# Layer 1 of a four-layer convolution-style kernel: first pieces loaded as attention drains, fifteen shared slots, planes stored raw and scaled by selecting products

## The chip, the cores and the metric

The kernel runs on one core of one Trainium2 chip. The metric is device time in microseconds (us) for one execution, lower is better. The engines are named as the profile names them: PE (matrix products; PEld is its weight load), DVE, ACT and POOL (elementwise work; ACT has the lookup functions), and SP, which issues most DMAs. "SPq", "POOLq" and so on are the queues of instructions of those engines.

## The reference

The input x is 1x256x256x128 f32. Four layers follow each other; each is `x = x + layer(_gn(x))`, where `_gn` is a group normalisation over 32 groups of 4 channels and the whole image. Layer 0 is an attention over rows with a triangle bias, layer 2 a gated triangle product over 128 channels, layer 3 a chain of small convolutions. The change is in layer 1, a gated triangle product over 16 channels:

```python
def _L1_conv_ref(x, Wa1, ba1, ..., Wz, bz):
    a = sigmoid((x @ Wa1 + ba1) * (x @ Wa2 + ba2))      # 256x256x16
    b = sigmoid((x @ Wb1 + bb1) * (x @ Wb2 + bb2))      # 256x256x16
    g = sigmoid(x @ Wg + bg)                            # 256x256x128
    z = einsum('bikc,bkjc->bijc', a, b)                 # per channel a 256x256 product
    return g * (_ln(z, ln2_g, ln2_b) @ Wz + bz)         # _ln over the 16 channels
```

## The kernel before, in words

All intermediate images lie in DRAM with the channel first: x1T (the input of layer 1), x2T (its output), abD (32 rows: 16 planes of a and 16 of b), znD (16 normalised planes of z). A token is one pixel; 65,536 tokens are cut into 32 pieces of SC = 2048 tokens, a piece into four chunks of CK = 512. A piece of x1T is an SBUF tile of 128 channels x 2048 tokens, 1 MB.

**Attention (layer 0)** works in 64 groups of four image rows, in a hand-written order (a `manual_schedule` loop over j). `gate` (L611) multiplies the gate in, takes the reciprocal of the softmax sums and sends it through DRAM (rzD) to spread it over the heads (L625, L628, issued by SP), `divide` (L636, POOL) multiplies, `output` (L643, L644) makes the new x, and `close` (L648, L650) takes bn_stats and stores the group to x1T by SP. The exponentials live in a pool p2e (six tiles of 8 KB per partition and five of 4 KB), which is opened after the pools p2c and p2.

**Between attention and layer 1** an aggregate of all statistics (L777) makes a flag, which every engine reads and branches on (`tc.If`, L787; the branch holds a slower attention for unusual numbers). Then `gn_finish` aggregates once more (L200) and folds the group normalisation into the weights of layer 1 (L207 to L219, L807 to L815). Only then are pieces of x1T loaded.

**Planes (L820 to L838).** For each piece in order: load (L824, SP), eight products that put four chunks into the four 32-partition quarters of a PSUM tile (L829), an Identity on ACT (L834), a fused multiply on DVE (L835), a Sigmoid on ACT (L837), and one store of 256 KB into abD by POOL (`store_groups`, L172). Eight of the 32 pieces stay in SBUF (`held`); the others go through three slots.

**Multiply (L850 to L893).** For each of 16 channels: load planes a and b in groups of four channels (L859, L861), turn a by four transposes (`tri_turn`, L1718, with a copy by ACT, L1720), multiply (`tri_multiply`, L1729), subtract the first plane (L870, DVE), square (L872, ACT), and add the sum and the sum of squares on POOL (L877, L878). All 16 results stay in SBUF. Afterwards variance, root and reciprocal (L882 to L886) give one factor per token, which scales all planes (L889, DVE, four instructions); then they are stored to znD (L890).

**Gating (L895 to L950).** For each piece: two halves of the gate product (L927) with a Sigmoid each (L930, ACT), four products of the normalised planes with Wz, each reading 16 partitions (L935), a fused add and multiply (L941, DVE, twice), the residual add on POOL (L944), then four bn_stats (L910, DVE) for the next group normalisation and the store to x2T (L911, SP). `fetch_zn` (L903) loads the normalised planes for four pieces in four transfers into 16 partitions each. Pieces that were not held are loaded again (L846), seven slots in all.

The time line of SP matters: it issues its DMAs in program order, and waits at each for the slot, the data or an earlier transfer.

The group normalisation that follows (`gn_finish(stats2)`) aggregates 128 statistics; layer 2 begins with loads of x2T (L999).

Of the kernel before, what the change touches and what calls it, by code (L numbers as in the profile page):

```python
# [9 lines left out]
F32 = mybir.dt.float32  # L10
AF = mybir.ActivationFunctionType
ALU = mybir.AluOpType
# [20 lines left out]
def kernel(ctx: ExitStack, tc: tile.TileContext, a: dict, out: bass.AP):  # L33
# [47 lines left out]
    cen4 = const.tile([P, 4, 32], F32, name="f1_c")  # L81
    nc.vector.memset(cen4, -1.0 / 16)
    for q in range(4):
        for sign, base in ((1, -32 * q), (-1, 32 * q + 31)):
            nc.gpsimd.affine_select(
                out=cen4[:, q, :], in_=cen4[:, q, :], compare_op=ALU.is_ge, fill=0.0, base=base,
                pattern=[[0, 32]], channel_multiplier=sign,
            )
    nc.vector.tensor_tensor(cen4.rearrange("p q c -> p (q c)"), cen4.rearrange("p q c -> p (q c)"), ident, ALU.add)
# [45 lines left out]
    wz4 = const.tile([P, D], F32, name="wz4")  # L135
    nc.vector.memset(wz4, 0.0)
    g4 = const.tile([P, 1], F32, name="g4")
    nc.vector.memset(g4, 0.0)
    for q in range(4):
        nc.gpsimd.dma_start(wz4[32 * q : 32 * q + 16, :], a["L1_conv_Wz"])  # L140
        nc.gpsimd.dma_start(g4[32 * q : 32 * q + 16, :], a["L1_conv_ln2_g"].unsqueeze(1))
# [28 lines left out]
    def store_groups(queue, dst, s, src):  # L170

        queue.dma_start(dst[:, s * SC : (s + 1) * SC].rearrange("c (q t) -> q c t", q=4), src)  # L172

# [23 lines left out]
    def gn_finish(stats, name):  # L197

        mv = const.tile([P, 2], F32, name=name + "_mv")
        nc.vector.bn_aggr(mv, stats.rearrange("p n s -> p (n s)"))  # L200
        return gn_groups(mv, name)

    def gn_groups(mv, name):
# [40 lines left out]
    wzc = const.tile([P, D], F32, name="wzc")  # L244
# [4 lines left out]
    with tc.tile_pool(name="x0", bufs=1) as xres, tc.tile_pool(name="p0", bufs=3) as sb:  # L249
        held = {s: xres.tile([P, SC], F32, name=f"x0_{s}") for s in range(RES, NSC)}  # L250
        with tc.tile_pool(name="p0ps", bufs=3, space=PSUM) as ps, tc.tile_pool(
# [12 lines left out]
            def folds():  # L264
# [37 lines left out]
                pw = fps.tile([P, D], F32, name="f1_w", tag="f0")  # L302
                nc.tensor.matmul(pw, lhsT=cen4.rearrange("p q c -> p (q c)"), rhs=wz4, start=True, stop=True)
                yield
                nc.vector.tensor_copy(wzc, pw)
# [186 lines left out]
    with tc.tile_pool(name="p2c", bufs=1) as cs:  # L492
        triT = cs.tile([P, NH, 2, N], F32, name="triT")
        with tc.tile_pool(name="p2", bufs=2) as sb, tc.tile_pool(name="p2e", bufs=6) as eb, tc.tile_pool(
# [117 lines left out]
            def gate(i0):  # L612
# [10 lines left out]
                nc.vector.reciprocal(rz, t["z"])  # L623
                for h in range(NH):
                    nc.sync.dma_start(rzD[g, h * G : (h + 1) * G, :], rz[h * HC : h * HC + G, :])  # L625
                rb = sb.tile([P, GT], F32, name="p2_rb")
                for h in range(NH):
                    nc.sync.dma_start(  # L628
                        rb[h * HC : (h + 1) * HC, :],
                        rzD[g, h * G : (h + 1) * G, :].rearrange("r n -> (r n)").unsqueeze(0).to_broadcast([HC, GT]),  # L630
                    )
# [14 lines left out]
            def close(g, c):  # L646
                x1 = groups[g]["x"]
                nc.vector.bn_stats(stats1[:, g * 2 + c, :], x1[:, c * CK : (c + 1) * CK])  # L648
                if c == 1:
                    nc.sync.dma_start(x1T[:, g * GT : (g + 1) * GT], x1)  # L650
                    del groups[g]
# [60 lines left out]
            for j in range(2 * NG + 5):  # L712
# [55 lines left out]
                if half == 0 and 0 <= g - 2 < NG:  # L768
                    divide(g - 2)
                if half == 1 and g + 2 < NG:  # L770
                    prepare(g + 2)


    flag = const.tile([P, 1], mybir.dt.int32, name="flag")
    with tc.tile_pool(name="chk", bufs=1) as sb, tc.tile_pool(name="chkps", bufs=1, space=PSUM) as ps:
        mv = sb.tile([P, 2], F32, name="chk_mv")
        nc.vector.bn_aggr(mv, stats1.rearrange("p n s -> p (n s)"))  # L777
        ok = sb.tile([P, 2], F32, name="chk_ok")
        nc.vector.tensor_scalar(ok, mv, 0.0, 0.0, ALU.mult, ALU.is_equal)
# [6 lines left out]
    with tc.If(again > 0):  # L786
# [4 lines left out]
        )  # L791

    layer0.close()
    m1, r1 = gn_finish(stats1, "gn1")

    v1 = const.tile([P, 32], F32, name="v1")
# [16 lines left out]
    stats2 = new_stats("stats2")  # L816
    R1 = 8
    with tc.tile_pool(name="x1", bufs=1) as xres, tc.tile_pool(name="xs1", bufs=3) as xsb:
        held = {s: xres.tile([P, SC], F32, name=f"x1_{s}") for s in range(0, NSC, NSC // R1)}
        with tc.tile_pool(name="p3", bufs=3) as sb, tc.tile_pool(name="p3ps", bufs=3, space=PSUM) as ps:  # L820
            for s in range(NSC):
                ss = slice(s * SC, (s + 1) * SC)
                xt = held[s] if s in held else xsb.tile([P, SC], F32, name="p3_x", tag="xs")
                nc.sync.dma_start(xt, x1T[:, ss])  # L824
                p1 = ps.tile([P, CK], F32, name="p3_1")
                p2 = ps.tile([P, CK], F32, name="p3_2")
                for pp, w in ((p1, v1), (p2, v2)):
                    for c in range(4):
                        nc.tensor.matmul(  # L829
                            pp[32 * c : 32 * c + 32, :], lhsT=w, rhs=xt[:, c * CK : (c + 1) * CK],  # L830
                            start=True, stop=True,
                        )
                s1 = sb.tile([P, CK], F32, name="p3_s1")
                nc.scalar.activation(s1, p1, AF.Identity, bias=vb1)  # L834
                nc.vector.scalar_tensor_tensor(s1, p2, vb2, s1, ALU.add, ALU.mult)  # L835
                ab = sb.tile([P, CK], F32, name="p3_ab", bufs=10)
                nc.scalar.activation(ab, s1, AF.Sigmoid)  # L837
                store_groups(nc.gpsimd, abD, s, ab)  # L838

        loaded = {}  # L840

        def fetch1(pool, tag, bufs):
            for s in range(NSC):
                if s not in held and s not in loaded:
                    loaded[s] = pool.tile([P, SC], F32, name="p4_x", tag=tag, bufs=bufs)
                    nc.sync.dma_start(loaded[s], x1T[:, s * SC : (s + 1) * SC])  # L846
                    return


        with tc.tile_pool(name="z", bufs=1) as zb, tc.tile_pool(name="zs", bufs=2) as sb, tc.tile_pool(  # L850
            name="zps", bufs=2, space=PSUM
        ) as ps:
            Z = zb.tile([P, 16, 2 * N], F32, name="Z")
            s1 = zb.tile([P, 2 * N], F32, name="z_s1")
            s2 = zb.tile([P, 2 * N], F32, name="z_s2")
            base = zb.tile([P, 2 * N], F32, name="z_base")
            for q in range(4):
                A = sb.tile([P, 4, 2 * N], F32, name="z_A")
                nc.sync.dma_start(A, abD[4 * q : 4 * q + 4, :].rearrange("c (p t) -> p c t", p=P))  # L859
                B = sb.tile([P, 4, 2 * N], F32, name="z_B")  # L860
                nc.sync.dma_start(B, abD[16 + 4 * q : 20 + 4 * q, :].rearrange("c (p t) -> p c t", p=P))  # L861
                for c in range(4):
                    at = tri_turn(nc, ps, sb, A, c, ident, nc.scalar.copy)
                    pz = tri_multiply(nc, ps, at, B, c).rearrange("p t n -> p (t n)")
                    k = 4 * q + c
                    if k == 0:
                        nc.vector.tensor_copy(base, pz)
                        nc.vector.memset(Z[:, 0, :], 0.0)
                        continue
                    nc.vector.tensor_tensor(Z[:, k, :], pz, base, ALU.subtract)  # L870
                    sq = sb.tile([P, 2 * N], F32, name="z_sq", bufs=3)
                    nc.scalar.activation(sq, Z[:, k, :], AF.Square)  # L872
                    if k == 1:
                        nc.gpsimd.tensor_copy(s1, Z[:, k, :])
# [896 lines left out]
```

## Time and profile before

| what | value |
|---|---|
| runs of the kernel, median of 4 | 3441.0 us (3435.27 to 3448.64) |
| profiled execution, its own time | 3431.01 us |
| profiled execution, span | 3429.3 us |
| mean granted PE clock | 0.958 |
| busy share PE / DVE / ACT / POOL | 91% / 68% / 57% / 48% |
| last bn_stats of attention ends | 1478.2 us |
| first product of the planes | 1499.6 us |
| first load of the multiply stage | 1610.6 us |
| last plane of z subtracted | 1658.2 us |
| first fused multiply of the gating | 1688.3 us |
| last store of layer 1 landed | 1864.6 us |

The last six rows are times from the start of the span in the profiled execution. Layer 1 thus takes about 386 us from the end of attention to the landing of its last store, 11% of the span. In the profile's groups a line gives the instruction's line and engine, the tile it writes and those it reads, the shape, the number of instructions, their busy time and mean duration, and how long the engine was idle just before them and what ended that. In the chain of waits, each step is followed back to what released it. "issue" is time in which the engine waited for nothing that the profile shows.

### The profile page before, as it was taken

Reading aid. Unit: us, or ns where it says so; the run is one execution under the profiler, and the core shown is the slowest. Engines: PE = TensorE matmul, PEld = TensorE weight load, DVE = VectorE, ACT = ScalarE, POOL = GpSimd, SP = SyncE. Lnnn points to the kernel's source line nnn. Section 1 sums busy time; section 2 is a strip of 40 time slices with the busy share of each in tenths; the row PEclk is TensorE's granted clock in tenths of the full one; section 3 lists DMA queues with packets and bytes.
Section 4 is the critical chain, followed back from the end, with each engine's and each line's share of the span. In section 5 each row is a group of like instructions: output and inputs, shape, how many; then the busy total and the mean of one; then the engine's idle time right before and its main releaser. Section 6 shows DMA issues by size and latency. Waiting matters only on the chain.

```text
span 3429.3 us, 52490 instructions
## 1 busy us (share of the span) xinstructions
PE 3113.6 (91%) x20266; PEld 1646.4 (48%) x20266; DVE 2318.3 (68%) x2635; ACT 1954.9 (57%) x2140; POOL 1650.4 (48%) x914
## 2 busy tenths in 40 slices
PE   6669999999999999955696999999999999859998
PEld 5425555555555555512432444444899533324444
DVE  5627888888888888831596445544555677747876
ACT  3657777777777777623343444543444466736555
POOL 4146777777777777721595000000555344514433
PEclk8889999999999999988898999999999999979999
DMA  9982333333333333279699676856999899856764
GB/s 391 358 292 80 118 117 110 119 106 120 111 119 107 118 114 111 95 271 346 194 324 355 233 273 250 311 217 232 344 351 350 307 336 334 305 161 196 208 198 130
DMA packets 302409, 755.31 MB, mean 220 GB/s; under 512 B 79577, under 2 KB 150139, under 8 KB 252363
## 3 DMA queue, kind: packets, MB, share of 16 engines
q1 hardware_dynamic: 288235, 741.02, 61.7%
q0 software_dynamic: 13920, 10.87, 1.1%
q8 instruction: 162, 2.65, 0.3%
q14 instruction: 92, 0.75, 0.1%
HBM read 464.09 MB, written 287.66 MB: 219 GB/s over the span
## 4 chain that ended last, share of the span: by engine, by line
PE 41%; DMA 9%; DVE 2%; issue 1%; ACT 1%; POOL 1%; SPq 0%; ACTq 0%; DVEq 0%; POOLq 0%
PE p_pm L1063 13%; PE tp_z L1729 7%; PE p_pm L1216 6%; PE p_pm L1451 5%; DMA p_x<-x1T 2%; DMA abD<-p_ab 2%; PE tp_a L1718 2%; DMA p_er<-eD 2%; DMA x2T<-p_x 2%; PE p_st L1020 1%; PE p_pt L1488 1%; PE p_eb L977 1%; PE p_rz L977 1%; PE p_rk L977 1%; PE p_pp L1344 1%
## 5 line engine op out<-in xcount | busy, mean ns | idle before, releaser
L575 DVE TENSOR_TENSOR p_e<-p_S,triT 128x1024 f32<-128x1024 f32 x512 | 609.4, 1212 | 144.4 <-PE p_S L565 144.4
L585 POOL TENSOR_TENSOR p_es<-p_e 128x1024 f32<-128x1024 f32 x256 | 602.9, 2366 | 125.6 <-issue 66.6
L583 ACT ACTIVATE p_e<-p_e,mbT 128x1024 f32<-128x1024 f32 x512 | 552.2, 1138 | 60.5 <-DVE p_e L575 60.3
L1063 PE MATMUL p_pm<-p_zn,wf 128*128 128x512 f32 x1040 | 450.8, 595 | 1.4 <-DVE p_zn L1080 1.4
L550 PE MATMUL p_mm<-p_xn,w 128*128 128x512 f32 x768 | 404.9, 610 | 0.3 <-DVE p_v L545 0.3
L1063 PEld LDWEIGHTS p_pm<-p_zn,wf 128*128 128x128 f32 x1040 | 197.8, 191 | 255.1 <-issue 248.3
L565 PE MATMUL p_S<-p_q,p_k 32*128 32x256 f32 x4096 | 295.1, 400 | 3.5 <-DVE p_e L575 3.3
L1465 POOL TENSOR_TENSOR p_q<-p_q,p_pb 128x2024 f32<-128x2024 f32 x32 | 144.1, 4504 | 251.3 <-DVE p_pb L1459 242.5
L565 PEld LDWEIGHTS p_S<-p_q,p_k 32*128 32x128 f32 x4096 | 185.9, 184 | 159.5 <-PE p_mm L541 91.7
L1129 POOL DMA_DIRECT2D rs__17885<-rs2D x4 | 2.0, 512 | 532.3 <-PE p_pm L1063 532.3
L1729 PE MATMUL tp_z<-p_B,tp_at 128*128 128x256 f32 x1024 | 250.7, 388 | 2.5 <-DMA p_B<-bD 2.2
L524 POOL TENSOR_TENSOR p_xn<-p_xn,p_rs 128x1024 f32<-128x1024 f32 x63 | 151.2, 2400 | 204.6 <-DMA p_rb<-rzD 122.8
L598 PE MATMUL p_o<-p_e,p_v 128*32 128x256 f32 x4096 | 247.6, 382 | 0.0
L1172 POOL TENSOR_TENSOR k<-k,p_sq 128x512 f32<-128x512 f32 x128 | 163.1, 1274 | 135.3 <-ACT p_sq L1170 135.3
L1282 POOL TENSOR_TENSOR p_x<-p_x,p_g 128x2048 f32<-128x2048 f32 x30 | 136.3, 4544 | 160.5 <-DVE p_g L1269 106.9
L1729 PEld LDWEIGHTS tp_z<-p_B,tp_at 128*128 128x128 f32 x1024 | 185.3, 191 | 25.2 <-issue 2.6
L550 PEld LDWEIGHTS p_mm<-p_xn,w 128*128 128x128 f32 x768 | 125.8, 190 | 104.3 <-issue 88.3
L1171 DVE TENSOR_TENSOR k<-tp_z,k 128x512 f32<-128x512 f32 x128 | 88.5, 692 | 129.0 <-ACT p_sq L1170 129.0
L598 PEld LDWEIGHTS p_o<-p_e,p_v 128*32 128x32 f32 x4096 | 120.0, 109 | 109.3 <-ACT p_g L556 41.5
L1096 DVE SCALAR_TENSOR_TENSOR p_b<-p_pm,b2w,p_b 128x1024 f32<-128x1024 f32 x64 | 82.2, 1284 | 125.6 <-PE p_pm L1063 111.2
L1168 ACT COPY p_K<-tp_z 128x512 f32<-128x512 f32 x128 | 74.9, 585 | 159.8 <-PE tp_z L1729 159.8
L541 PEld LDWEIGHTS p_mm<-w,p_xn 128*128 128x128 f32 x1024 | 134.4, 191 | 61.1 <-issue 60.1
(367 smaller groups left out, 5924.5 us busy)
## 6 DMA issues: line engine op xcount, KB each, us to landing
p_x<-x2T SPq DMA_DIRECT2D x64, 1024.0 KB
p_x<-x1T SPq DMA_DIRECT2D x48, 1024.0 KB
p_x<-in_x_dram SPq DMA_DIRECT2D x32, 1024.0 KB
p_x<-xT SPq DMA_DIRECT2D x64, 512.0 KB
p_rb<-rzD SPq DMA_DIRECT2D x256, 128.0 KB
x1T<-p_x SPq DMA_DIRECT2D x64, 512.0 KB
aD<-p_a SPq DMA_DIRECT2D x32, 1024.0 KB
bD<-p_b SPq DMA_DIRECT2D x32, 1024.0 KB
```

Source lines behind the costliest of these rows:

```text
L524: nc.gpsimd.tensor_tensor(xn, xn, groups[g]["rs"], ALU.mult)
L550: nc.tensor.matmul(pm, lhsT=w, rhs=t["xn"][:, cs_], start=True, stop=True)
L565: nc.tensor.matmul(Ss[h // 2][:, h % 2, u, :], lhsT=t["k"][hp, r * N + u * P : r * N + (u + 1) * P], rhs=t["q"][hp, r * N : (r + 1) * N], ...
L575: nc.vector.tensor_tensor(e[:, :, 2 * p : 2 * p + 2, :].rearrange("p u h n -> p h u n"), Ss[p], triT[:, 2 * p : 2 * p + 2, :, :], ALU.add,)
L583: nc.scalar.activation(e[:, u, :, :], e[:, u, :, :], AF.Exp, bias=mbT[:, u, i : i + 1])
L585: nc.gpsimd.tensor_tensor(es, e[:, 0, :, :], e[:, 1, :, :], ALU.add)
L598: nc.tensor.matmul(t["o"][hp, r % 2, :], lhsT=t["v"][:, r * 2 + u, hp], rhs=e[:, u, h, :], start=(u == 0), stop=(u == 1),)
L1063: nc.tensor.matmul(pm[:, c, :], lhsT=wf2[:, i, :], rhs=zns[s][:, k * CK : (k + 1) * CK], start=True, stop=True)
L1172: nc.gpsimd.tensor_tensor(k2, k2, sq, ALU.add)
L1216: nc.tensor.matmul(pm[:, c, :], lhsT=w, rhs=src[:, k * CK : (k + 1) * CK], start=True, stop=True)
L1451: nc.tensor.matmul(pm[:, 2 * c : 2 * c + 2, :], lhsT=w2c, rhs=src[:, r : r + 2, :], start=True, stop=True)
L1729: nc.tensor.matmul(pz[:, t, :], lhsT=at[:, u, t * P : (t + 1) * P], rhs=Bc[:, u, :], start=(u == 0), stop=(u == 1))
```

## The change

It does five things.

1. **Attention's end.** The pool p2e is opened first, so that it lies lowest. The last group's reciprocals and the last two groups' stores are issued by ACT instead of SP. The statistics of all groups but the last are aggregated inside the loop (`gn_part`), and merged with those of the last group by five small operations (`gn_merge`); flag and normalisation use the merged values. The first eight pieces of x1T are loaded ahead of the flag, into a pool that lies where p2e was.
2. **Slots.** Fifteen slots of 1 MB (KEEP = 10 and MORE = 5) hold pieces in planes, multiply and gating. Ten pieces stay from the planes on, five are loaded during the multiply, 17 during the gating, into a slot whose piece was stored. The order of the pieces alternates between the image's halves: 0, 16, 1, 17 and so on (`order1`).
3. **Planes.** The order is written by hand, with the Sigmoid one piece late. A piece is stored by four transfers of 32 partitions, two issued by POOL and two by SP, in another order of the tokens in abD, so that partition 32 q + s of a loaded plane holds chunk q of piece s.
4. **Multiply.** Planes come in groups of two channels, three groups ahead; the next plane is turned before the present one is multiplied; the sum goes to DVE (the sum of squares stays on POOL, the last on DVE). Each result is stored raw as soon as it is there.
5. **Gating.** The raw planes of four pieces are fetched in two transfers into 128 partitions. The factor per token is spread by small products with a selecting matrix (`spread`, eight products of 32x32 per four pieces), and a DVE multiply scales the planes. Statistics for the next normalisation come from the fused multiply's accumulation (DVE) and from a Square with accumulation on ACT, instead of bn_stats. For six of the pieces the residual add is done by DVE instead of POOL. Gates run two pieces ahead.

The core of the diff (the constants for Wz, with eight blocks of 16 rows instead of four, are cut):

```diff
-    with tc.tile_pool(name="p2c", bufs=1) as cs:
+    with tc.tile_pool(name="p2e", bufs=6) as eb, tc.tile_pool(name="p2c", bufs=1) as cs:
...
+                queue = nc.sync if g < NG - 1 else nc.scalar
                 for h in range(NH):
-                    nc.sync.dma_start(rzD[g, h * G : (h + 1) * G, :], rz[h * HC : h * HC + G, :])
+                    queue.dma_start(rzD[g, h * G : (h + 1) * G, :], rz[h * HC : h * HC + G, :])
...
+                    queue = nc.sync if g < NG - 2 else nc.scalar
+                    queue.dma_start(x1T[:, g * GT : (g + 1) * GT], x1)
...
+                if j == 2 * NG + 2:
+                    mv_first = gn_part(stats1, 0, 2 * NG - 2, "gn1_a")
...
+    order1 = [b + h * NSC // 2 for b in range(NSC // 2) for h in range(2)]
+    KEEP, MORE, FIRST = 10, 5, 8
...
+    for i in range(FIRST):
+        load1(i, x1_pool)
+    mv1 = gn_merge(mv_first, gn_part(stats1, 2 * NG - 2, 2 * NG, "gn1_b"), 1.0 - 1.0 / NG, "gn1_mv")
...
+            def store3():
+                s, ab = done.pop(0)
+                for q in range(4):
+                    (nc.gpsimd if q < 2 else nc.sync).dma_start(
+                        abD.rearrange("c (q s t) -> q s c t", q=4, t=CK)[q, s], ab[32 * q : 32 * q + 32, :]
+                    )
...
+                for k in range(16):
+                    if k and k % 2 == 0:
+                        load_z(k // 2 + 2)
+                    nxt = turn_z(k + 1)
+                    pz = tri_multiply(nc, ps, at, AB[k // 2][1], k % 2).rearrange("p t n -> p (t n)")
+                    at = nxt
...
+                            nc.vector.tensor_tensor(s1, s1, Z, ALU.add)
+                            (nc.vector if k == 15 else nc.gpsimd).tensor_tensor(s2, s2, sq, ALU.add)
...
+                            nc.sync.dma_start(znD[k_].rearrange("(p t) -> p t", p=P), Z_)
...
+                    if k % 2 == 1 and KEEP + k // 2 < KEEP + MORE:
+                        load1(KEEP + k // 2, xs_pool)
...
+                def scale_z(i):
+                    if i < NSC:
+                        rb = psg.tile([P, 2, CK], F32, name="p4_rb", tag="p4_pg")
+                        for m in range(2):
+                            for c in range(4):
+                                q = slice(32 * c, 32 * c + 32)
+                                nc.tensor.matmul(
+                                    rb[q, m, :], lhsT=spread[q, order1[i] + m, :], rhs=s1[q, :], start=True, stop=True
+                                )
+                        nc.vector.tensor_tensor(zs[i], zs[i], rb, ALU.mult)
...
+                def sum4():
+                    i = sums.pop(0)
+                    nc.scalar.activation(
+                        junk, xs[order1[i]], AF.Square, bias=c1neg, accum_out=qsum[:, i : i + 1]
+                    )
...
+                for i, s in enumerate(order1):
+                    xt = xs[s]
+                    if i:
+                        gate4(i + LEAD)
+                    if i % 4 == 0:
+                        fetch_z(i + 8)
+                    if i % 4 == 2:
+                        scale_z(i + 2)
...
+                            pzh if i in by_dve else gt[:, hs], pzh, bz, gt[:, hs], ALU.add, ALU.mult,
+                            accum_out=usum[:, 2 * i + h : 2 * i + h + 1],
...
+                    sums.append(i)
+                    if len(sums) > 1:
+                        sum4()
+                    if i:
+                        s_ = order1[i - 1]
+                        nc.sync.dma_start(x2T[:, s_ * SC : (s_ + 1) * SC], xs[s_])
+                    j = i - 3 + KEEP + MORE
+                    if i > 2 and j < NSC:
+                        load1(j, x1_pool if j % (KEEP + MORE) < KEEP else xs_pool)
```

## The prediction

> **What bounds layer 1 now.** I read the 40 slices first, then the busy time by stage, the groups between 1485 and 1870 us, the chain of waits, and the time line around each seam. All times are of the profiled execution: span 3429.3 us, time 3431.01 us. The median of the four runs is 3441.0, so I work out a difference and take it off both. A difference under 0.3% (10 us) counts as no change.
>
> Busy time by stage (PE, PEld, DVE, ACT, POOL, then granted clock, DMA share, GB/s):
>
> ```profile
> 1468.00:1500.00 32.00, 6.52 (x32) 3.73 (x36) 13.10 (x21) 1.54 (x2) 2.34 (x1) 0.58 0.48 178
> 1500.00:1592.00 92.00, 64.28 (x512) 17.08 (x504) 21.78 (x29) 38.29 (x60) 19.33 (x28) 0.94 1.01 388
> 1592.00:1616.00 24.00, 0.36 (x4) 0.02 (x1) 2.74 (x4) 3.24 (x6) 2.83 (x5) 0.58 0.82 280
> 1616.00:1658.00 42.00, 38.95 (x192) 33.60 (x192) 10.86 (x16) 16.83 (x30) 32.92 (x28) 0.96 0.48 167
> 1658.00:1685.00 27.00, 3.70 (x8) 1.44 (x8) 15.32 (x9) 5.77 (x6) 2.84 (x3) 0.67 0.50 169
> ...
> 1700.00:1796.00 96.00, 95.86 (x331) 35.59 (x329) 96.00 (x122) 45.48 (x42) 91.37 (x21) 1.00 0.98 326
> ```
>
> Three seams hold no bulk work: before the first planes (1468 to 1500), between planes and multiply (1592 to 1616), and between multiply and gating (1658 to 1685). The planes stage is bound by DMA (share 1.01), the multiply by PE (38.95 of 42). In the gating stage PE, DVE, POOL and DMA are all full. The chain of waits (start, us, what) shows what fills the seams:
>
> ```profile
> 1597.98 12.38 DMA abD<-p_ab
> ...
> 1663.44 3.36 DVE z_s L886
> 1666.82 8.91 DVE Z L889 x4
> 1675.75 5.86 DMA znD<-Z
> ...
> 1681.82 3.18 DMA p_zn<-znD
> ```
>
> The last store of the planes, then reciprocal, scaling, store and reload of the normalised planes, one after the other. The prices of the gating stage:
>
> ```profile
> L944 POOL TENSOR_TENSOR p_x<-p_x,p_g 128x2048 f32<-128x2048 f32 x24 | 108.7, 4530 | 20.6 <-DVE p_g L941 19.3 <-DMA x2T<-p_x 1.0 <-DMA p_x<-x1T 0.2
> L941 DVE SCALAR_TENSOR_TENSOR p_g<-p_pz,bz,p_g 128x1024 f32<-128x1024 f32 x64 | 78.9, 1274 | 30.0 <-ACT p_g L930 16.5 <-DMA p_zn<-znD 12.6 <-PE p_pz L935 0.9
> L930 ACT ACTIVATE p_g<-p_pg,bgf 128x1024 f32<-128x1024 f32 x64 | 71.2, 1114 | 97.2 <-PE p_pg L927 97.2
> ```
>
> **Attention's end.** Now the first planes product starts at 1499.6. The last bn_stats ends at 1478.2; two aggregates over all statistics (L777, L200: 3.6 us each) and the flag's branch stand between. In the change the big aggregate runs earlier, in POOL's wait of 5.95 us for the last reciprocals (DVE is idle too). What remains is a 12-element aggregate and five small operations at 0.16 to 0.22 us, some 1.3 us. The flag comes at 1480.7, the branch ends at 1482.7, and the row from the group product (1488.7) to the last folded bias (1494.0) adds 5.3: 1488. The eight loads sit on SP behind the store of group 61, issued at 1459.7; their slots lie over tiles of p2e, whose last readers end at 1463.2. 8.4 MB at 400 GB/s take 21 us, so the pieces are there by about 1482. But they share the engines with the last group's reciprocals (stored from 1465.0, reloaded by 1470.7, now issued by ACT, which is idle). Bounds: 0, and 5.7, that round trip doubled. I take 3: first product 1491. If the loads gave no lead, the 21 us would come back in the planes stage.
>
> **Planes.** Products cost 1.92 us a piece, so 32 need 62 us; DMA decides. After the branch 24 loads and 8.4 MB of stores are left, 33.6 MB. At the 1500 to 1592 rate for a mix of this kind (about 400 GB/s in its middle) that is 84 us from 1485: 1569. Two unknowns. A store is now four transfers of 32 partitions, two by POOL and two by SP, where SP's stand behind up to five loads; the five ab buffers then hold up only ACT, two pieces from where PE would feel it (three PSUM buffers). The price of 32 partitions is not in the trace. Nearest: loads of zn into 16 partitions, 1 MB in 1681.8 to about 1690, some 120 GB/s; whole tiles reach 400 and more. Stores at 120 would take 70 us instead of 21 (+49), at best +0; I take +4, since half the transfers run beside the loads on another queue. The last load then lands at 1573. Its product, two activations and a multiply cost 4 us, the last stores 6 (now 12.4, from POOL alone and with a median of 18.2 us to landing): the multiply stage begins at **1583** instead of 1610.6, bounds 1576 and 1628.
>
> [...]
>
> **Multiply.** Turning and multiplying cost 4.2 us of PE per two planes plus 0.6 waiting for ACT's copy. Turning a plane ahead removes the 0.6: 34 us. DMA now carries planes 8.4 MB, raw planes 3.9 and five pieces of x1 5.2: 17.5 MB, 44 us. So it becomes DMA-bound: 46 us with the first landing, as long as now (1610.6 to 1657.5). The sums' move to DVE (0.7 a plane; L882 took 1.74 beside POOL where L1240 took 0.68, so up to 1.05 more) stays below 2.8 a plane. Last plane 1629. Then sums, variance, root (0.7+0.7+1.7+0.7+0.4+0.7) and reciprocal 3.36: 1638. Scaling (8.9) leaves; store and reload lie beside that chain. Late next is ACT: the root is ready at 1635, table load 1.28, six sigmoids at 1.11 with products between, to 1645.6; then selecting product 1.9 (like L829's 16 instructions), scaling multiply 1.2, plane product 0.6, two fused multiplies 2.5. First piece done at **1651**, against 1691.7 now.
>
> **Gating.** Now 31 pieces from 1691.7 to 1854.1: 5.24 us each. Removed: 128 bn_stats (0.55 each pipelined) and the 16-partition fetches. Added on ACT: a Square with accumulation, 2.0+0.19 by L1229; ACT 4.4 us a piece. Six pieces add on DVE (2×1.21 in place of POOL's 4.53). DVE's accumulation is not in the trace: 0 to 0.19 (ACT's reading row) per instruction, off DVE's limit either way. DMA: 17 loads, 32 stores and 4.2 MB of planes, 55.6 MB at 400, 139 us, under the rest. On SP each store waits for POOL's add and the load behind it for a store to land; what queues there is fetched 12 pieces ahead (some 60 us), so nobody waits for it. The copies that make the spread tile (two, on POOL) lie in POOL's idle time after the last planes store, and cost 1 to 2 us without it.
> Floor by PE: gates 3.63 and plane products 1.07 (the time line shows plane products 4.70 us apart), seven more selecting products at 1.92: 29×3.63+31×1.07+13.4 = 152 us, 4.9 a piece.
> Loop by order: Square of a piece waits for POOL's add; behind it on ACT stand the next sigmoids, behind them, through two PSUM buffers, the selecting product, and then that piece's multiply. From one piece's end to the next but one: 4.53+2.19+1.11+1.92+1.22+2.46 and 0.5 of hand-overs = 13.9 us. It holds for every fourth piece; with 4.15 and 4.7 for the other two, 22.8 per four: 5.7 a piece. Without the selecting product the loop spans three pieces, 15.1, or 5.0. DVE's six adds shorten it at some places. I take 5.5, nearer the loop: 31×5.5 = 170.5, 1821.5. The last piece's adds 2.4, its store 5.9 (as now): **1830**. Now 1864.6. The end statistics (Square 2.2, two reductions) lie beside the 12.3 us of the next stage's first load, as the aggregate does now. Eight more weight transfers at 0.53 us on POOL at the start lie under the 32 input pieces; 0 to 4 us without that cover.
>
> **Sum.** 1864.6−1830 = 34 us: 3397 against the profile's 3431, 3407 against the median.
>
> **Rivals.**
> 1. PE's floor holds (4.9): 15 to 19 us less, gain 51, 3390. For it: PE runs at 4.70 now whenever data is there. Against: the new wait of ACT on POOL.
> 2. Narrow stores bind the planes stage: at the upper bound +45, so 1628 and 3452, at half of that 3429; I set it between, at 3440. For: the 120 GB/s row. Against: two queues. [...]
> 3. The eight loads wait for the whole pool and start after the branch: 20 us back, 3427. Against: the slots lie over p2e alone.
> 4. Slower: ACT's Square decides at every piece, not every fourth. The 13.9 us loop over two pieces is 7.0 each; 31×7.0 = 217, end at 1876, 3453. It passes the old time from 6.6 a piece, and would show as ACT waiting on POOL, PE below 75%.
>
> **Numbers.** Forecast 0.46, rival 1 0.25, rival 2 0.08, rival 3 0.08, rival 4 0.13. Faster: forecast, rival 1, most of rival 3 and a part of rival 2: 0.81; same 0.06; slower 0.13. The range goes from 3370 (floor, and stores at no extra cost) to 3440 (rivals 2 and 3); rival 4 and the ends are left out.
>
> **What would show it.** Right: x1 loads landing before 1485, multiply from about 1583, first fused multiply near 1649, pieces 5.5 us apart with ACT waiting for POOL's add. Wrong: DMA share near 1 with under 330 GB/s in the planes stage (rival 2), or pieces 6.6 us apart (rival 4).

## The result, and the profile after

| kernel | median us (runs) | ratio to before, 95% interval |
|---|---|---|
| before | 3439.79 (65) | 1 |
| after | 3434.53 (40; 3423.82 to 3442.71) | 0.9983 (0.9977 to 0.9989) |

The change gains about 6 us (0.17%), where 34 were forecast. That is inside what the text of the prediction calls no change. The two profiled executions taken alone would have said the opposite (3431.01 us before, 3435.47 after, span 3433.7): the one of before lies 8.8 us under its median, and layer 3, which is not touched, differs between them by some 6 us. So I compare the traces by the duration of stages within layer 1, and the kernels by their medians. Attention ahead of layer 1 also ends at slightly different times in the traces. Where the end of layer 1 is compared, I count from the issue of the store of group 61, the last store of x1T that SP issues in attention (1458.9 in after, 1456.5 to 1466.3 in the others).

Milestones of layer 1, in us from the start of the span:

| milestone | before | forecast | after |
|---|---|---|---|
| last bn_stats of attention starts | 1477.5 | | 1477.1 |
| first load of x1 issued by SP | 1487.8 | about 1460 | 1479.8 |
| first product of the planes | 1499.6 | 1491 | 1507.1 |
| multiply's first load | 1610.6 | 1583 | 1597.2 |
| last plane's subtraction starts | 1657.5 | 1629 | 1649.4 |
| first product of normalised planes | 1685.1 | | 1673.2 |
| last product of normalised planes starts | 1850.9 | | 1851.5 |
| last store landed | 1864.6 | 1830 | 1861.3 |

Read by differences: the first product comes 7.5 us *later* than before, the planes all the same end 13.4 earlier, the multiply keeps 8.1 of this, the gating begins with 11.9 in hand. From its first product to its last it then takes 178.3 us, where the old one took 165.8. Most of what the first three stages gain is given back in the fourth.

The busy time by stage, with the columns of the table shown in the prediction:

```profile
1468.00:1507.00 39.00, 6.37 (x28) 3.51 (x28) 10.94 (x27) 1.54 (x2) 2.34 (x1) 0.54 0.68 266
1507.00:1592.00 85.00, 64.18 (x512) 16.53 (x512) 23.22 (x32) 37.95 (x63) 28.73 (x58) 0.93 0.95 376
1592.00:1601.00 9.00, 0.00 (x0) 0.00 (x0) 0.80 (x2) 1.51 (x3) 3.69 (x8) 0.60 0.70 198
1601.00:1650.00 49.00, 39.54 (x192) 33.46 (x192) 20.87 (x31) 17.20 (x30) 16.10 (x13) 0.93 0.90 344
1650.00:1673.00 23.00, 15.31 (x40) 5.76 (x40) 7.82 (x8) 10.49 (x10) 0.41 (x1) 0.85 0.24 81
1700.00:1796.00 96.00, 88.73 (x337) 31.41 (x335) 52.66 (x78) 70.01 (x69) 63.18 (x15) 1.00 0.99 384
```

The seam before the planes has grown (39 us with 6.37 of PE), the seam between planes and multiply is nearly gone, and the multiply is now bound by DMA (0.90) and not by PE. The last line is the one to look at longest: DVE fell from 96.00 to 52.66 us and POOL from 91.37 to 63.18, yet PE, the engine that should now set the pace, fell too, from 95.86 to 88.73. Something makes it wait.

The seam before the planes, in the time line (start, us, engine, line, what; in brackets the idle time before it and what ended that):

```profile
1477.08 0.69 DVE L638 BATCH_NORM_STATS2 stats<-p_x 128x6 f32<-128x512 f32 x1
...
1479.84 28.24 SPq L778 DMA_DIRECT2D x<-x1T  x15
...
1489.44 0.16 DVE L200 COPY gn_mean<-gn_pm 128x1 f32<-128x1 f32 x1 [6.80 <-PE gn_pm L198]
...
1503.76 0.16 DVE L202 TENSOR_TENSOR gn_d<-gn_mv,gn_mean 128x1 f32<-128x1 f32 x1 [14.16 <-SPq L795]
...
1507.06 9.45 PE L859 MATMUL p<-x,v 128*32 128x512 f32 x64 [0.25 <-DVE bgf L826]
```

The loads (L778) are issued 2.8 us after the last bn_stats starts, not 17 before it. Then a 0.16 us subtraction on one column stands still for 14.16 us, and what ends its wait is SP's queue at L795, the branch of the flag.

The seam between multiply and gating, and the gating's loop, in the chain of waits:

```profile
1654.21 3.36 DVE z_s L942
1657.71 1.28 ACT L985
1659.00 1.12 ACT p_g L985
...
1660.17 9.76 PE p_pg L982 x16
...
1677.04 4.53 POOL x L1033
1681.61 1.89 issue
1683.50 0.19 ACT p_junk L992
1683.68 1.01 ACT p_g L985
...
1684.74 2.47 PE p_rb L969 x16
```

The last five lines are the loop that the prediction described: POOL's add, the Square (1.89, shown as "issue", and its accumulator's reading, 0.19), a sigmoid, the selecting products. The chain takes the add, the Square and a sigmoid four more times; from 1753 to 1829 it runs through POOL's adds instead, once by way of a slot's store and load.

### The profile page after: what moved, and what is told of

The parts are those of the page before. It is cut to its first block, busy times and chain, and to the rows that moved or that the text cites. A ratio compares the mean times of both kernels' runs of the same rounds, so it can differ in the third digit from the quotient of the medians.

```text
span 3433.7 us, 52984 instructions
## 1 busy us (share of the span) xinstructions
PE 3134.7 (91%) x20394; PEld 1648.2 (48%) x20394; DVE 2264.3 (66%) x2612; ACT 2015.5 (59%) x2204; POOL 1618.5 (47%) x928
## 4 chain that ended last, share of the span: by engine, by line
PE 42%; DMA 6%; POOL 2%; DVE 2%; issue 2%; ACT 1%; SPq 0%; ACTq 0%; POOLq 0%; DVEq 0%
PE p_pm L1167 13%; PE tp_z L1833 7%; PE p_pm L1320 6%; PE p_pm L1555 5%; POOL x L1033 2%; PE tp_a L1822 2%; DMA abD<-p_ab 2%; PE p_st L1124 1%; PE p_pt L1592 1%; DMA p_er<-eD 1%; PE p_eb L1081 1%; PE p_rz L1081 1%; PE p_pg L982 1%; PE p_rk L1081 1%; PE p_pp L1448 1%
## 5 line engine op out<-in xcount | busy, mean ns | idle before, releaser
L545 ACT ACTIVATE p_g<-p_mm,bgh 128x512 f32<-128x512 f32 x128 | 88.0, 687 | 131.4 <-PE p_mm L539 131.3
```

## The experiments

The theory from these traces had four separate losses, each with an edit that removes it: (1) the subtraction that waits at the branch, because its scratch column shares its place with something that the loads write; (2) the late start of the loads; (3) the five loads of x1 in the DMA-bound multiply; (4) the Square that waits for POOL. Rivals: a stage that is bound by something else and swallows the edit (DMA in the planes, which take 42 MB whatever the start), and a loss that only moves on. All ratios are to the kernel before, run beside them.

| run | what | median us | ratio, 95% interval |
|---|---|---|---|
| after | the change | 3434.53 | 0.9983 (0.9977 to 0.9989) |
| e1_scratch | own scratch columns | 3435.07 | 0.9994 (0.9983 to 1.0005) |
| e2_split | x1 pool of 8 + 2 slots | 3427.42 | 0.9973 (0.9963 to 0.9983) |
| e3_late_loads | the five loads after the multiply | 3426.87 | 0.9969 (0.9955 to 0.9983) |
| e4_square | Square one piece later | 3415.89 | 0.9940 (0.9926 to 0.9955) |
| e5_all_four | e1 to e4 together | 3400.75 | 0.9888 (0.9873 to 0.9904) |
| e6_no_early_loads | no load ahead of the flag | 3431.68 | 0.9978 (0.9968 to 0.9988) |
| e8_pool_loads | e2, e3, e4, early loads by POOL | 3404.49 | 0.9898 (0.9883 to 0.9913) |
| e9_late_and_square | e6, e3, e4 | 3409.25 | 0.9913 (0.9899 to 0.9928) |
| e12_ab12 | twelve ab buffers | 3428.32 | 0.9985 (0.9966 to 1.0004) |
| e10_all_five | e5 and e12 | 3394.94 | 0.9875 (0.9859 to 0.9891) |
| e17_four_early | e10 with four early loads | 3408.65 | 0.9912 (0.9898 to 0.9925) |

**e1_scratch: the subtraction's wait.**

```diff
-    d = sb.tile([P, 1], F32, name=name + "_d")
+    d = (const if name == "gn1" else sb).tile([P, 1], F32, name=name + "_d")
```
(and the same for `sd`.)

> Edit: the two scratch columns of the folded normalisation lie in a pool of their own instead of above the x1 pool. Theory A (two placement waits, the order of the multiply's loads and the order of ACT's Square took the gain): the 14.2 us in which DVE stood before the scratch column's first write go, the first planes product starts near 1494 instead of 1507, but the eight loads still start at 1480; the multiply's first load near 1588 instead of 1597.7, the kernel 9 us faster than with the whole change. Theory B (the stage is bound by the bytes moved from 1480 on, so waits only change places): the multiply's first load within 3 us of 1597.7, the kernel within 3 us.

The time line of this kernel:

```profile
1487.22 0.16 DVE L202 TENSOR_TENSOR gn_d<-gn_mv,gn_mean 128x1 f32<-128x1 f32 x1
...
1490.15 0.15 DVE L826 TENSOR_TENSOR bgf<-L_conv_bg_sb,f_g 128x1 f32<-128x1 f32 x1 [0.34 <-PE f_g L825]
1501.75 2.23 PE L859 MATMUL p<-x,v 128*32 128x512 f32 x8 [11.64 <-SPq L795]
```

The subtraction no longer waits, the weights are folded by 1490.3, and then the first product waits 11.64 us for the same releaser. The edit is a miss in time: nothing is gained (0.9994; the interval touches that of after). It still tells the cause: not the column is late but everything that is ordered behind SP's branch. SP's own branch instruction takes 0.05 us, at 1482.8. Eight waits follow it, and they end one after the other while the eight loads land:

```profile
L795 SPq EVENT_SEMAPHORE  x8: 17/17/17, 1486.6 to 1501.6; - x8
```

The branch's other arm loads the same eight pieces again, also by SP. The runs do not tell whether the branch alone or this second load brings the eight waits.

**e2_split: why the loads start late.** The pool of ten slots takes 80 KB of each partition, p2e had 68 KB. In after, SP's queue waited before its first loads for the last group's reciprocals and the last bn_stats (total us, times, longest). Their tiles lie in p2 and not in p2e:

```profile
SPq L778 <- DMA p_rb<-rzD: 10.5, 3, 9.6
...
SPq L778 <- DVE stats L638: 7.8, 1, 7.8
```

```diff
-    x1_pool = x1_scope.enter_context(tc.tile_pool(name="x1", bufs=KEEP))
+    x1_pool = x1_scope.enter_context(tc.tile_pool(name="x1", bufs=FIRST))
...
+    late_pool = x1_scope.enter_context(tc.tile_pool(name="x1b", bufs=KEEP - FIRST))
```

> Edit: the ten-slot pool (80 KB per partition) is cut into eight slots (64 KB, under the 68 KB of the exponentials' pool) and a second pool of two that is opened after the branch. Theory A: the first load is issued near 1460 instead of 1479.8, all eight are there by about 1484, the wait before the scratch column shrinks from 14.2 us to 0 to 2; first planes product near 1491, the multiply's first load near 1583, the kernel 14 us faster than with the whole change. Theory B: loads earlier, but the multiply's first load within 5 us of 1597.7, because the stores of the planes set the pace, and the kernel within 4 us.

```profile
1462.42 37.67 SPq L778 DMA_DIRECT2D x<-x1T  x12
...
1479.16 2.34 POOL L626 TENSOR_TENSOR p_u<-p_u,p_rb 128x1024 f32<-128x1024 f32 x1 [15.23 <-DMA p_rb<-rzD]
...
1486.15 0.69 DVE L638 BATCH_NORM_STATS2 stats<-p_x 128x6 f32<-128x512 f32 x1
```

The pool now takes 64 KB. The loads start at 1462.4, about as the prediction had it, and both waits are gone from the list (what is left before the first load is 3.1 us for PE's products of L597, which read p2e): the size of the pool was the cause. But now the last group's reciprocals come late. In the kernel after the same multiplication waits less than half as long:

```profile
1470.08 2.34 POOL L626 TENSOR_TENSOR p_u<-p_u,p_rb 128x1024 f32<-128x1024 f32 x1 [6.07 <-DMA p_rb<-rzD]
```

Eight loads of 1 MB beside 4 KB stores and 128 KB reloads cost 9.2 us at this place, and the last bn_stats starts 9.1 later. The first product is at 1499.6, the multiply's first load at 1591.1: 6 us won of the 14 that were missing, and 3.4 us of the median. A second loss stands behind the first: the eight loads have landed by 1492, but the ninth is not issued before 1498, and from 1490 to 1498 the DMA share is at most 0.13. SP's queue waits there for DVE:

```profile
SPq L778 <- DVE v L818: 5.9, 1, 5.9
```

**e6_no_early_loads: what the early loads are worth.**

```diff
-    KEEP, MORE, FIRST = 10, 5, 8
+    KEEP, MORE, FIRST = 10, 5, 0
```

> Edit: no piece is loaded ahead of the flag; all first pieces are loaded behind the branch. Theory A (eight loads in flight across the branch can be used only when SP has settled all its transfers there, so they bring nothing): the wait before the scratch column goes, the loads start near 1484 instead of 1480, the first product near 1495 instead of 1507, the multiply's first load within 4 us of 1597.7, the kernel within 4 us of the whole change. Theory D (the early loads are worth their lead of 8.4 MB): 15 to 20 us slower than the whole change.

Without them the first product comes at 1491.8, 15.3 us earlier than after: nothing is in flight at the branch, its other arm loads no pieces, and SP's eight waits are over by 1484.3; the multiply's first load comes at 1598.0, against 1597.2. So as they stand the early loads bring nothing and cost nothing. The rest of the stage is bound by DMA in both; the 50 us from 1540, first of this kernel, then of after:

```profile
1540.00:1590.00 50.00, 31.16 (x264) 7.93 (x256) 12.00 (x16) 18.73 (x32) 15.73 (x32) 1.00 1.01 415
```

```profile
1540.00:1590.00 50.00, 31.90 (x257) 8.12 (x253) 12.01 (x16) 18.15 (x31) 15.55 (x32) 0.97 1.01 414
```

From 1485 to 1598 the kernel without early loads moves 42 MB, which at 400 GB/s are 105 us. After's lead of 8.4 MB is used up at 1500 to 1540, where its DMA share falls to 0.70, 0.77 and 0.88 in three of the four stretches of 10 us.

**e12_ab12: are the stores' buffers the thin place?** ACT waits for ab buffers in the planes stage, which could hold up the products and with them the loads.

```diff
-                ab = sb.tile([P, CK], F32, name="p3_ab", bufs=5)
+                ab = sb.tile([P, CK], F32, name="p3_ab", bufs=12)
```

> Edit: twelve ab buffers instead of five, on the whole change. Theory E (a store on SP stands behind up to fifteen loads, so the five buffers are held, ACT stops near 1516 and PE behind it, and DMA then runs dry): ACT's wait of 11 us near 1516 goes, DMA share between 1520 and 1540 rises from 0.83 to over 0.95, the multiply's first load 6 to 8 us earlier, the kernel 5 to 8 us faster than with the whole change. Rival F (the stage is at what DMA can move anyway, 42 MB at 420 GB/s from 1480): under 3 us.

The waits of ACT from 1505 to 1600 (total us, times, longest), after and then this kernel:

```profile
ACT p_ab L842 <- DMA abD<-p_ab: 39.1, 18, 6.1
```

```profile
ACT p_s L868 <- PE p L859: 46.0, 30, 3.9
```

The wait is gone whole, and another of the same size stands in its place: ACT now waits for products, and these for loads (PE's wait for x is 21.7 us, 18.1 in after). The ratio is that of after. In the trace the planes take a little less, 87.8 us from the first product to the multiply's first load instead of 90.1, with a DMA share of 0.96 and 0.89 in the two stretches from 1520 to 1540 instead of 0.77 and 0.88. So a wait of 39 us was worth some 2 us at most, as rival F said, and not the 5 to 8 of theory E.

**e3_late_loads: the multiply.**

```diff
-                    if k % 2 == 1 and KEEP + k // 2 < KEEP + MORE:
-                        load1(KEEP + k // 2, xs_pool)
+                    if k == 15:
+                        for i in range(KEEP, KEEP + MORE):
+                            load1(i, xs_pool)
```

> Edit: the five loads of x1 that lie between the multiply's planes are issued behind its last store. Theory A: the multiply loses 5.2 MB, 13 us of DMA, and is bound by PE: 42 us from its first load to its last subtraction instead of 52.5, the gating as before (those pieces are read only from its eighth piece on), the kernel 9 us faster than with the whole change. Theory B: what is taken from the multiply comes back where the gating waits for its planes behind those loads: within 3 us.

```profile
1600.00:1641.00 41.00, 37.29 (x192) 33.03 (x192) 20.28 (x30) 16.74 (x30) 16.22 (x15) 0.91 0.85 297
```

The stage takes 41.2 us (1599.8 to 1641.0) instead of 52.2, and PE is again what fills it (37.29 of 41). The five loads then run in the seam behind it, where after's DMA share is 0.24. Nothing is given back in the trace: counted from the store of group 61, the next layer's first load comes 11.5 us earlier. The medians show 4.8 us; the intervals of this kernel and after overlap, so the size is uncertain, the sign comes from the trace and from e9.

**e4_square: the gating.**

```diff
-                    if len(sums) > 1:
+                    if len(sums) > 2:
                         sum4()
...
+                sum4()
                 sum4()
```

> Edit: the Square with accumulation stands one piece later in ACT's order. Theory A: the loop add, Square, sigmoid, selecting product, fused multiply then spans three pieces where it spanned two (13.9 us over 3 = 4.6 a piece), PE's 4.9 decides: 31 pieces at 4.9 to 5.1 instead of 5.7, the kernel 19 to 22 us faster than with the whole change. Theory C (POOL's adds, or the slots' stores and loads, set the pace): 5.5 to 5.7 a piece, within 5 us.

The waits from 1690 to 1836 of after, then the busy time of 50 us in the middle of the gating for this kernel:

```profile
POOL x L1033 <- DVE p_g L1022: 52.3, 19, 8.9
...
ACT p_junk L992 <- POOL x L1033: 31.7, 21, 2.5
```

```profile
1740.00:1790.00 50.00, 49.76 (x198) 17.57 (x196) 26.99 (x40) 40.23 (x39) 38.85 (x9) 1.00 0.98 365
```

The Square's wait for POOL (31.7 us, 21 times) is down to 0.5 us, the sigmoid behind it now waits 8.4 us for POOL, and PE is busy for 49.76 of 50 us, against 46.80 in the same stretch of after. In after the selecting products, which close the loop, start 22.8 to 24.4 us apart from the second on; the loop as forecast was 22.8. Here they start 20.8 to 22.1 us apart, and PE's own work for four pieces is 4×4.70 + 1.92 = 20.7. From the first product of the planes to the end of the 30th piece's it takes 154.2 us instead of 168.8. That is 14.6 us in the trace, and 14.8 by the medians' ratios (0.0043 of 3440). One line in another place is worth more than twice what the whole change gained. It is still less than the 19 to 22 us expected: by the prediction's own measure, from the first piece done to the last, the gating takes 162.5 us here, 5.24 a piece, as long as before the change (162.4).

**e5_all_four.**

> Edit: the four edits of the first four experiments together. Theory A, as it stands after them (the waits lie in series, so what each gave alone adds up, by the traces: 6 us at the multiply's start from the split pool, 11 in the multiply, 14 in the gating): the last store of layer 1 is issued near 1826 instead of 1856, the kernel 28 to 32 us faster than with the whole change. Theory B (time gained early is given back by DMA in the gating): 15 to 20 us.

0.9888: 38 us under before, 33 under after, a little more than expected. By where layer 1 ends in the traces, counted from the store of group 61, the four edits alone give 1.2 + 8.1 + 11.5 + 15.0 = 36 us over after, and this kernel gives 33.7: the losses were nearly separate. The parts do not act quite alone: the wait of 5.9 us for DVE that stood behind e2 is not there when e1's scratch columns are added, and the multiply's first load comes 4 us earlier than in e2 by the same count, though e1 alone had brought nothing. By medians the parts alone give −3.8 + 3.4 + 4.8 + 14.8 = 19. The five intervals together leave some 12 us either way around the difference to 33, so the medians do not tell whether the parts only add or also help each other.

**e9_late_and_square** takes the simple way: no early loads, the five loads late, the Square late.

> Edit: no early loads, late loads of the multiply, late Square. Theory A: 22 to 26 us faster than the whole change (11 in the multiply, 14 in the gating, 0 to 3 lost at the start). Theory D: 5 to 10 us.

0.9913. Its parts alone (e6 −1.7, e3 −4.8, e4 −14.8 against after) make 21.3; measured are 24, as theory A had it. Against e5, early loads that start in time are worth 8.6 us by the medians, but the intervals overlap; the traces say 7.3.

**e8_pool_loads: the early loads from another queue**, so that SP has nothing in flight at the branch and, if the queue was the cause, the reciprocals are not held up.

```diff
     for i in range(FIRST):
-        load1(i, x1_pool)
+        load1(i, x1_pool, nc.gpsimd)
```

> Edit: the split pool, the late loads of the multiply and the late Square as before, and the eight early loads are issued by POOL, whose queue reaches them behind the division that waits for the last reciprocals. Theory A: the reciprocals' two trips are undisturbed again (POOL's wait near 6 us instead of 15), the loads start near 1473 and are there by 1496, the first product near 1496, the multiply's first load 3 to 5 us earlier than with the loads on SP; the kernel 30 to 35 us faster than with the whole change. If POOL's own transfers of 1 MB are slow, the first product is later than 1500 and the kernel slower than with all four edits.

0.9898 is 29 us under after and not told apart from e5; the mechanism was missed. POOL's multiplication by the last reciprocals still waited 11.65 us, with four of the loads issued ahead of it in POOL's order. Nor was SP free at the branch: the last of its eight waits ended at 1496.2, though SP itself had no load in flight. The DMA share was 1.00 until 1495 and 0.09 after it, so these waits fit loads of another queue just as well.

**e10_all_five** has e5 and the twelve buffers of e12.

> Edit: the four edits and twelve ab buffers. Theory E: 4 to 7 us faster than the four edits alone (3401 us), near 3396. Rival F: within 3 us of 3401.

The fastest of all: 0.9875 (0.9859 to 0.9891), 3394.94 us against 3434.75 for before beside it. The intervals do not tell it apart from e5; the traces, counted from the store of group 61, differ by 2.5 us.

**e17_four_early: fewer early loads**, so that less stands beside the reciprocals.

```diff
-    KEEP, MORE, FIRST = 10, 5, 8
+    KEEP, MORE, FIRST = 10, 5, 4
```

> Edit: as the last one, with four early loads instead of eight. If the early loads take more from the last group's reciprocals (POOL's wait 15.2 us with eight, 6.1 without) than they give, four are better: POOL's wait 9 to 11 us, last bn_stats 4 us earlier, the kernel 1 to 4 us faster than with eight. If their lead is worth more than the delay, 1 to 4 us slower.

```profile
1486.52 2.34 POOL L626 TENSOR_TENSOR p_u<-p_u,p_rb 128x1024 f32<-128x1024 f32 x1 [15.15 <-DMA p_rb<-rzD]
```

A miss on both counts. Four loads hold the reciprocals as long as eight (15.57 us in e10), and the kernel is 13 us slower than e10, since DMA stands nearly idle (shares 0.22, 0.19, 0.11) from 1485 to 1500. What fits is that the delay does not come from the bytes queued ahead: the reciprocals landed at 1486, with four loads just as these were ending, with eight while they ran on to about 1497. What causes the delay instead, no run here shows.

## Why the prediction was wrong

The mechanisms were mostly named rightly, but several steps failed, and nearly all in the same direction. In the profile of after the last store landed at 1861.3 instead of 1830. The 31 us, by the prediction's own steps:

| step | forecast | measured | us late |
|---|---|---|---|
| up to the multiply's first load | 1583 | 1597.7 (start of its transfer in the chain) | +14.7 |
| multiply | 46 | 51.7 | +5.7 |
| last plane to first piece | 22 | 27.5 | +5.5 |
| gating | 170.5 | 177.0 | +6.5 |
| tail | 8.5 | 7.3 | −1.2 |

- **"Their slots lie over tiles of p2e, whose last readers end at 1463.2"** failed, and with it "the slots lie over p2e alone", the argument against rival 3. The pool is 12 KB per partition larger than p2e, and its first tile waited for all that lay under the whole pool. I had taken the pool's place from the diff and not its size. e2 shows it. Rival 3's mechanism (0.08) thus happened in part: the loads waited for the whole pool, but they started ahead of the branch, at 1479.8.
- **"The flag comes at 1480.7, the branch ends at 1482.7"** holds for DVE (1482.5 after), but not for SP, which had the loads in flight. This wait was in no rival. e1 and e6 show it together: with loads in flight the first product waits until they have landed (11.64 us in e1), without them it comes at 1491.8. It does not hold for PE either. PE's own branch instruction takes 3.91 us in before, where it ends before DVE's second aggregate and so costs nothing; the forecast kept it at nothing. In after it takes 6.77 us, and the group product, which the forecast puts right behind the branch, starts at 1488.8:

```profile
L795 PEldq COMPARE_BRANCH  x1: 6766/6766/6766, 1481.8 to 1481.8; - x1
```

  In e6 it takes 4.13 us. That e6 comes so near my 1491 is therefore luck: PE's branch, passed 3.7 us later than DVE's, stands in the place of the 3 us taken for the reciprocals, and the row behind it takes 4.0 us instead of 5.3, because its table load (1.28) is done before.
- **"Bounds: 0, and 5.7 … I take 3"** for the reciprocals beside the loads: in after it was 0.1, because the loads came too late to disturb; where they came in time (e2) it was 9.2. The upper bound was too low: POOL's wait for that round trip went from 6.07 us (after) to 15.23 (e2).
- **"84 us from 1485"** had the DMA full without a break. It was full at 1540 to 1590 (1.01, 414 GB/s), and at 0.90 with 335 GB/s from 1507 to 1540, 0.56 with 163 GB/s in the last 8 us. e2 shows that loads in time do not suffice: its DMA stands still for some 8 us between the eighth load and the ninth.
- **The multiply, "DMA-bound: 46 us"**: right in kind, 5.7 short in size. The mean was 337 GB/s and not 400: 393 from 1611 to 1645, but 106 in the first 3 us, 156 from 1607 to 1611 and 113 in the last 5 us. e3 shows the cause by taking the loads out.
- **"First piece done"**, 22 us after the last plane: the root was ready in time, but the table load of the sigmoids, put right behind the root, waited until the reciprocal was done (it starts at 1657.71, 0.15 us after the reciprocal's end, and does so in e3, e4, e5, e9 and e10 too): 3.5 us. The 16 gate products behind it took 9.76 us where two pieces at 3.63 make 7.3; PE had idled for 6.3 us, and its granted clock was 0.50 from 1660 to 1665 and 0.95 in the next 5 us: 2.5 more. Neither was tried by itself.
- **Gating, "I take 5.5, nearer the loop"**: the loop's 5.7 was the right number; measured 177.0/31 = 5.71 a piece. The loop was worked out correctly, place and price (22.8 us per four pieces), and then lowered, because DVE's six adds were to shorten it; no interval between selecting products in the loop is shorter than 22.8 us. e4 takes the loop away. This one choice cost 6 us of the miss. At 5.71 a piece, as at the 5.5 forecast, the gating is *slower* than the old 5.24; from first to last product it gives back 12.5 us of what the other stages had won.
- **Rival 2** (narrow stores) is refuted. Half of each piece's stores run beside the loads, and the mix went at 414 GB/s (after, 1540 to 1590). The row for 16 partitions alone (120 GB/s) did not carry over to a mix.
- **The store's landing time** fell from a median of 18.2 us to 5.2, for transfers of a quarter of the old size; what of this is due to the size and what to the new cut of the store, no run shows. The 6 us forecast for the last stores were an estimate that no run shows: in after the last of them landed 3.3 us after the last sigmoid of the planes (1593.82 to 1597.10). The issues in the window from 1485 to 1612, with size and median us to landing, before and then after:

```profile
abD<-p_ab POOLq DMA_DIRECT2D x32, 256.0 KB, 18.2
```

```profile
abD<-p_ab POOLq DMA_DIRECT2D x64, 64.0 KB, 5.2
```

- **Rival 4** (Square decides at every piece) is refuted: 5.71 and not 7.0 a piece. **Rival 1** was right that PE decides once the Square is moved (e4), but its 152 us are not reached, 162.5 are. Its 4.9 a piece spread 29 gates over 31 pieces; while gates run, a piece costs PE 5.2 us, and the last two pieces, put at 1.07 each, took 12.0 us together.

Put together, the time forecast, 3407, is near what the change gives with no early loads and two of its waits taken out (e9: 3409.25). The plan was worth it, ahead of the gating: there e5 takes 162.5 us as well, no less than before the change. Four places in the code, each of a few lines, had taken the gain away.

## What to carry to other kernels

When a plan starts transfers early, look at two things that no row of the old profile shows: how large the pool is that they land in (in after its first tile waited for all that lay under the whole pool, to 1479.8 where the smaller one of e2 had its first load at 1462.4), and which branch they will be in flight across (11.64 and 14.16 us of wait behind it here). An instruction that was hidden behind another may also stand alone in the new order, as PE's branch did (6.77 us in after). When a loop by order has been worked out to its last term, forecast that number, and then look whether one instruction can move out of the loop: here a Square one piece later was worth 15 us. And a wait in a list is no gain until the one behind it is known: here one of 39 us was replaced by one of 46, and the scratch columns of e1, worth nothing alone, paid once e2 had taken the wait ahead of them.

## What the runs showed of the hardware that I had not expected

- In after and e1, what this program orders behind SP's branch started only when the eight 1 MB loads in flight there had landed: 14.16 us of wait for the subtraction in after, 11.64 for the first product in e1, and no such wait without the loads (e6, where SP's eight waits are over by 1484.3).
- PE's branch instruction took 6.2 to 6.8 us in after, e1, e3, e4, e8 and e12, where the eight loads were still landing, and 3.8 to 4.4 us in before, e2, e5, e6, e9, e10 and e17, where none were left or the last were landing. On DVE, ACT, POOL and SP it took 0.05 to 0.07 us.
- Where the last group's small transfers (4 KB, then 128 KB) ran beside 1 MB loads of another queue, POOL waited 15 us for them instead of 6: 15.15 with four loads (e17), 15.23 and 15.57 with eight (e2, e10), 6.07 where the loads came later (after).
- In after, each of DVE's 64 accumulating instructions of L1022 is followed by a second one that reads the accumulator. It took 83 ns behind the 52 that write SBUF and 142 ns behind the 12 that write PSUM:

```profile
L1022 DVE DVE_READ_ACCUMULATOR p_g<-p_pz,bz,p_g 128x1 f32 x52 | 4.3, 83 | 0.0
...
L1022 DVE DVE_READ_ACCUMULATOR p_pz<-p_pz,bz,p_g 128x1 f32 x12 | 1.7, 142 | 0.0
```

**Left open:** why four early loads delay the reciprocals as much as eight; whether the waits at the branch come from the branch or from the loads in its other arm; why PE's branch takes so long; whether the twelve buffers add to e5 beyond the 2.5 us of one trace; and how much of the 27.5 us between last plane and first piece would go if the sigmoids' table load did not wait for the reciprocal.
